# A four-layer image network: involution by columns of tiles and direct 3x3 convolutions, in place of involution by rows of tiles and convolutions by minimal filtering F(4,3)

## The chip, the core and the metric

One of the eight cores of a Trainium2 chip runs the whole network in one program. The metric is the time of that program on the device in microseconds. A core has five engines, each with its own queue of instructions in order: TensorE (PE, matrix products into PSUM; its weight loads are shown as PEld), VectorE (DVE), ScalarE (ACT), GpSimd (POOL) and SyncE (SP, which here only issues transfers). Sixteen DMA engines move data. Tiles live in SBUF, 128 partitions wide. All data is fp32.

## The reference

The image batch `x` is 4 x 256 x 56 x 56. Four layers follow one another, each as `x = x + layer(group_norm(x))`, with 32 groups of 8 channels. Layers 0 and 2 are involutions: a 1x1 bottleneck to 64 channels and a 1x1 span to 16 groups x 49 taps gives every pixel and every group of 16 channels its own 7x7 filter, which is applied to the normalised image. Layer 1 is a block of two 3x3 convolutions of 256 channels. Layer 3 is a gate over a Fourier sum.

```python
# layers 0 and 2 (2 has batch norms and a relu around the same core)
h = jnp.einsum('bchw,oc->bohw', x, reduce_w) + reduce_b[None, :, None, None]
kern = jnp.einsum('bchw,oc->bohw', h, span_w) + span_b[None, :, None, None]
kern = kern.reshape(b, G, 1, K * K, Ho, Wo)
out = (kern * patches).sum(axis=3)          # patches: 7x7 neighbourhoods, pad 3
# layer 1
h = _conv3x3(x, w1, stride=1)
h = jax.nn.relu(_bn(h, g1, b1, rm1, rv1))
h = _bn(_conv3x3(h, w2, stride=1), g2, b2, rm2, rv2)
return jax.nn.relu(x + h)
```

## The kernel before

**Involution** (`involution_layer`, called for layers 0 and 2). The image is cut into tiles of `TY` x `TX` = 3 x 8 output pixels, 19 rows of tiles (`NTY`) by 7 columns (`NTX`), 133 tiles in all (`NT`). A tile's patch has `QY` x `QX` = 9 x 14 = 126 pixels (`Q`). With the patch's 126 pixels on the partitions, the layer is a matrix product per tile: the patch (126 x channels) against a tap matrix (126 x 24 output pixels) for each group of channels.

For an image `b`, `prepare` loads both blocks of 128 channels, takes the statistics (`norm_stats`), and for each block and each column of tiles calls `strip`: ACT writes the normalised 14-pixel-wide strip (L274), PE transposes it in seven pieces of 9 rows (L287), ACT copies these out of PSUM (L290), and POOL's queue stores them to the DRAM scratch `xT` (L293). The seven pieces start at every third row of tiles only; the patches of the other rows of tiles begin inside a piece, which is why the strip goes through DRAM. Then the bottleneck's matmuls (L331) and ACT give `hp`.

`tap_matrices(b, cb)` builds the tile `kt` for one block `cb` of eight groups. It has 32 steps; a step is six matmuls of 64 x 126 weights by 133 columns (L368), three for each of two groups, into two PSUM tiles `k0`, `k1` of two buffers each. An eviction adds the bias and writes `kt`: of every eight PSUM tiles, ACT takes three in three instructions each (L385), DVE five in one each (L392).

`apply(b, cb, kt)` goes by rows of tiles. For each of the 19 rows SP's queue loads the seven patches `xw` from `xT` (L413, four buffers), PE does 7 x 4 matmuls of 126 x 32 weights by 48 columns (L417), and DVE (layer 0, L431) or ACT and DVE (layer 2, L437 to L443) add the result to the residual `res`, which is loaded again from DRAM (L409) and stored by POOL's queue (L445) every five rows of tiles.

The next image's `prepare` is woven by hand into `apply`: `weave` alternates two generators by their shares of steps. Within this order a scheduler places the instructions on the engines' queues, and pools with a fixed number of buffers make a writer wait until the readers of the old content are done.

**Convolutions** (`conv_layer`). They go by minimal filtering F(4,3) along the image's rows: four neighbouring output pixels from six input values take six products instead of twelve. The weights are transformed once (L489 to L499). For stripes of 18 to 20 image rows, `input1` and `input2` make the six transformed inputs on DVE (`transform`, 12 instructions per block), `products` multiplies them (6 products of 6 matmuls, L580) and combines them to four outputs on ACT and DVE (L592 to L603). `conv1` and `conv2` evict; `conv2` reloads the residual and stores the output.

**Gate** (`gate_layer`): as before and after.

Of the kernel before, what the change touches and what calls it, by code (L numbers as in the profile page):

```python
# [45 lines left out]
RES_TY = 5  # L46


WT, WPOS = W // 4, 6
CV_ROWS = 20  # L50
C1_ROWS = [(0, 20), (20, 38), (38, 56)]
C2_ROWS = [(0, 19), (19, 37), (37, 56)]
# [32 lines left out]
def net_kernel(  # L85
# [35 lines left out]

    xT = [dram.tile([NB, NTX, HS * QX, P], F32, name=f"xT{i}") for i in range(2)]
# [53 lines left out]

    def norm_stats(xb, mm_ps):
# [32 lines left out]
    def involution_layer(layer, xin, xout, red, span, sb):  # L210
        with ExitStack() as es:
# [6 lines left out]


# [5 lines left out]
            taps = work.tile([P, NB, KK * KK, GB], F32, name="taps", bufs=1)  # L225
# [15 lines left out]
            bias_g = work.tile([G, KK, KK], F32, name="bias_g", bufs=1)  # L241
# [3 lines left out]
            bias_f = work.tile([G, ZN], F32, name="bias_f", bufs=1)  # L245
# [14 lines left out]

            h_of = {}

            def strip(b, xs, rstd, shift, cb, tx):

                st = work.tile([P, HS, QX], F32, name="strip")
# [6 lines left out]
                if at + hi - lo < QX:  # L272
# [3 lines left out]
                    xs[:, cb, :].rearrange("p (h w) -> p h w", w=W)[:, :, lo:hi],  # L276
# [5 lines left out]
                xts = work.tile([Q, NSB, P], F32, name="xts")  # L282
                for k in range(0, NSB, 4):
                    n = min(4, NSB - k)
                    ps = mm_ps.tile([P, 512], F32, name="mm")
                    for i in range(n):
                        nc.tensor.transpose(  # L287
                            ps[:Q, i * P : (i + 1) * P], flat[:, (k + i) * Q : (k + i + 1) * Q], ident_sb
                        )
                    nc.scalar.copy(  # L290
                        xts[:, k : k + n, :], ps[:Q, : n * P].rearrange("q (n c) -> q n c", n=n)
                    )
                nc.gpsimd.dma_start(xT[b % 2][cb, tx].rearrange("(n q) c -> q n c", q=Q), xts)  # L293

            def prepare(b):

                xs = big.tile([P, NB, HW], F32, name="xs")
                for cb in range(NB):
                    nc.sync.dma_start(xs[:, cb, :], xin[b][cb])
                yield  # L300
                rstd, shift = yield from norm_stats(xs, mm_ps)

                redn = work.tile([P, NB, 2 * R], F32, name="redn")
# [15 lines left out]
                yield  # L319
                for cb in range(NB):  # L320
                    for tx in range(NTX):
                        strip(b, xs, rstd, shift, cb, tx)
                        yield

                hp = big.tile([P, TY, TX, NTY, NTX], F32, name="hp")
                nc.gpsimd.memset(hp[:, TY - 1, :, NTY - 1, :], 0.0)
                for j in range(-(-H // ROWS_H)):
                    rows = min(ROWS_H, H - j * ROWS_H)
                    ps = mm_ps.tile([P, 512], F32, name="mm")
                    for ci in range(NB):  # L330
# [3 lines left out]
                            xs[:, ci, j * ROWS_H * W : (j * ROWS_H + rows) * W],  # L334
# [16 lines left out]
                h_of[b] = hp  # L351


            PREP1, PREP2 = 1 + 2 * NCHUNK + 2 + 1 + NTX, NTX + 7

            def tap_matrices(b, cb):

                hp = h_of[b]
                kt = big.tile([Q, NT, GB, TP], F32, name="kt")
                n = 0  # L360
                for gp in range(GB // 2):
                    for pb in range(TP // PB):
                        ps = [k_ps.tile([P, 512], F32, name=f"k{i}") for i in range(2)]
                        for k in range(PB):
                            py, px = divmod(pb * PB + k, TX)
                            z0 = ZF - py * QX - px
                            for i in range(2):
                                nc.tensor.matmul(  # L368
                                    ps[i][:Q, k * NT : (k + 1) * NT],
                                    z_sb[  # L370
                                        i * R : (i + 1) * R,
                                        cb * GB // 2 + gp,
                                        z0 : z0 + Q,
                                    ],
                                    hp[i * R : (i + 1) * R, py, px].rearrange("p a t -> p (a t)"),
                                    start=True,
                                    stop=True,
                                )
                        for i in range(2):
                            gl = 2 * gp + i  # L380
                            g = cb * GB + gl
                            p0 = pb * PB
                            if n % 8 in (1, 4, 6):
                                for k in range(PB):
                                    nc.scalar.activation(  # L385
                                        kt[:, :, gl, p0 + k],
                                        ps[i][:Q, k * NT : (k + 1) * NT],
                                        AF.Identity,
                                        bias=zb_sb[:, g, p0 + k : p0 + k + 1],
                                    )  # L390
                            else:
                                nc.vector.tensor_tensor(  # L392
                                    kt[:, :, gl, p0 : p0 + PB].rearrange("q t k -> q k t"),
                                    ps[i][:Q, : PB * NT].rearrange("q (k t) -> q k t", k=PB),
                                    zb_sb[:, g, p0 : p0 + PB].unsqueeze(2).to_broadcast([Q, PB, NT]),
                                    ALU.add,
                                )
                            n += 1
                return kt

            def apply(b, cb, kt):

                xt = xT[b % 2]
                for c0 in range(0, NTY, RES_TY):
                    ntr = min(RES_TY, NTY - c0)
                    y0 = c0 * TY
                    rows = min(H, (c0 + ntr) * TY) - y0
                    res = work.tile([P, RES_TY * TY * W], F32, name="res", bufs=3)
                    nc.sync.dma_start(res[:, : rows * W], xin[b][cb][:, y0 * W : (y0 + rows) * W])  # L409
                    for ty in range(c0, c0 + ntr):  # L410
                        xw = work.tile([Q, NTX, P], F32, name="xw", bufs=4)
                        q0 = ty * TY * QX
                        nc.sync.dma_start(xw, xt[cb, :, q0 : q0 + Q, :].rearrange("t q c -> q t c"))  # L413
                        ps = o_ps.tile([P, 2, TY, W], F32, name="o")
                        for tx in range(NTX):
                            for j in range(GB // 2):
                                nc.tensor.matmul(  # L417
                                    ps[32 * j : 32 * j + 32, :, :, tx * TX : (tx + 1) * TX],
                                    xw[:, tx, 32 * j : 32 * j + 32],
                                    kt[:, ty * NTX + tx, 2 * j : 2 * j + 2, :].rearrange(  # L420
                                        "q g (y x) -> q g y x", y=TY
                                    ),
                                    start=True,
                                    stop=True,
                                )
                        n = min(TY, H - ty * TY)
                        xs = res[:, (ty - c0) * TY * W : ((ty - c0) * TY + n) * W]
                        o = [ps[:, i, :n, :].rearrange("p y w -> p (y w)") for i in range(2)]
                        if layer == 0:
                            for i in range(2):  # L430
                                nc.vector.scalar_tensor_tensor(  # L431
                                    xs, o[i], par_sb[:, i : i + 1], xs, ALU.mult, ALU.add
                                )
                        else:
                            u = work.tile([P, TY * W], F32, name="u", bufs=3)
                            un = u[:, : n * W]
                            nc.scalar.activation(  # L437
                                un, o[0], AF.Identity, bias=t4[:, cb : cb + 1], scale=s4p[:, 0, cb : cb + 1]
                            )
                            nc.vector.scalar_tensor_tensor(  # L440
                                un, o[1], s4p[:, 1, cb : cb + 1], un, ALU.mult, ALU.add
                            )
                            nc.vector.scalar_tensor_tensor(xs, un, 0.0, xs, ALU.max, ALU.add)  # L443
# [405 lines left out]
```

## Time and profile before

| | us |
|---|---|
| median of 3 runs | 2649.42 |
| lowest, highest | 2646.02, 2665.11 |
| the profiled execution | 2649.42 |
| its span, first to last instruction | 2647.6 |

The mean granted clock of TensorE is 0.857 of full speed. In the page's 40 slices of the span (66 us each, busy time in tenths), the layers can be told apart: slices 1 to 12 are layer 0, 13 to 25 the convolutions, 26 to 37 layer 2, the last three the gate.

```profile
PE   4777777777771999999999996587777677866422
DVE  2445644654565767667667564164365265445544
ACT  2435444444230412313313210355555455533311
PEclk8788889888785999999999998598888889877666
DMA  4385486568556101102101013327756945775353
```

The costliest groups (line, engine, operation, written tile, read tiles, shape, count; then busy us and mean ns of one; then idle time before them and who ended it):

```profile
L580 PE MATMUL mm<-v,u_sb 128*128 128x252 f32 (+2 forms) x3456 | 765.9, 384 | 5.7 <-DVE v L525 5.7
L368 PE MATMUL k<-hp,z_sb 64*126 64x133 f32 x6144 | 548.2, 302 | 100.2 <-DVE kt L392 67.4
L392 DVE TENSOR_TENSOR kt<-k,zb_sb 126x399 f32<-126x399 f32 x640 | 483.6, 832 | 216.3 <-PE k L368 207.4
L385 ACT ACTIVATE kt<-k,zb_sb 126x133 f32<-126x133 f32 x1152 | 378.8, 473 | 288.8 <-PE k L368 244.5
L417 PE MATMUL o<-kt,xw 126*32 126x48 f32 x17024 | 322.7, 235 | 205.6 <-issue 141.5
L287 PE MATMUL mm<-ident_sb,strip 128*126 128x128 f32 x784 | 174.1, 369 | 90.8 <-ACT xts L290 44.8
```

An fp32 matmul of the source appears as two records. A group's mean duration counts the overlap of pipelined neighbours; busy time over count is the pace. The transfers by queue (packets, MB, share of sixteen engines' span), and the two large issues (KB each, us to landing where the trace has it):

```profile
q1 hardware_dynamic: 293392, 246.69, 33.7%
q0 software_dynamic: 24192, 89.18, 10.3%
...
xw<-xT SPq DMA_DIRECT2D x304, 441.0 KB
xT<-xts POOLq DMA_DIRECT2D x112, 441.0 KB, 7.6
```

### The profile page before, as it was taken

What the parts mean: (1) busy time and instruction counts of PE and PEld (TensorE: products, weight loads), DVE (VectorE), ACT (ScalarE), POOL (GpSimd) and SP (SyncE); (2) the same over time, 40 slices, a digit from 0 to 9 for tenths busy, and PEclk for the clock granted to TensorE, in tenths of its full rate; (3) what the DMA queues carried; (4) which work ended last, traced back from release to release, by engine and by line L of the source; (5) the groups of instructions that cost most, each with busy time, mean ns of one, the idle gap of its engine ahead of it and who ended that gap; (6) DMA issues with size and microseconds to landing.
All of it is one profiled execution on the core that took longest, in us unless ns stands there. A gap on an engine that the chain in (4) does not pass through costs nothing. (4 is left out here: it accounts for less than half of the span.)

```text
span 2647.6 us, 63963 instructions
## 1 busy us (share of the span) xinstructions
PE 1993.9 (75%) x27984; PEld 1607.9 (61%) x27984; DVE 1433.6 (54%) x2911; ACT 958.7 (36%) x2158; POOL 295.4 (11%) x531
## 2 busy tenths in 40 slices
PE   4777777777771999999999996587777677866422
PEld 3556655665661788888888885465566466655100
DVE  2445644654565767667667564164365265445544
ACT  2435444444230412313313210355555455533311
POOL 2111011011001000000000000201101101100235
PEclk8788889888785999999999998598888889877666
DMA  4385486568556101102101013327756945775353
GB/s 127 124 202 160 145 229 185 140 182 228 124 142 194 49 17 66 65 17 74 57 33 65 1 34 116 110 79 213 198 141 168 249 130 163 193 176 139 151 197 145
DMA packets 325518, 346.15 MB, mean 131 GB/s; under 512 B 14483, under 2 KB 288115, under 8 KB 320627
## 3 DMA queue, kind: packets, MB, share of 16 engines
q1 hardware_dynamic: 293392, 246.69, 33.7%
q0 software_dynamic: 24192, 89.18, 10.3%
q10 hardware_dynamic: 7654, 6.19, 0.8%
q8 instruction: 220, 3.60, 0.6%
q14 instruction: 60, 0.48, 0.1%
HBM read 239.91 MB, written 102.06 MB: 129 GB/s over the span
## 5 line engine op out<-in xcount | busy, mean ns | idle before, releaser
L580 PE MATMUL mm<-v,u_sb 128*128 128x252 f32 (+2 forms) x3456 | 765.9, 384 | 5.7 <-DVE v L525 5.7
L580 PEld LDWEIGHTS mm<-v,u_sb 128*128 128x128 f32 x3456 | 655.0, 190 | 114.0 <-issue 5.7
L368 PE MATMUL k<-hp,z_sb 64*126 64x133 f32 x6144 | 548.2, 302 | 100.2 <-DVE kt L392 67.4
L392 DVE TENSOR_TENSOR kt<-k,zb_sb 126x399 f32<-126x399 f32 x640 | 483.6, 832 | 216.3 <-PE k L368 207.4
L368 PEld LDWEIGHTS k<-hp,z_sb 64*126 64x126 f32 x6144 | 463.8, 196 | 179.7 <-DVE kt L392 121.0
L385 ACT ACTIVATE kt<-k,zb_sb 126x133 f32<-126x133 f32 x1152 | 378.8, 473 | 288.8 <-PE k L368 244.5
L417 PE MATMUL o<-kt,xw 126*32 126x48 f32 x17024 | 322.7, 235 | 205.6 <-issue 141.5
L417 PEld LDWEIGHTS o<-kt,xw 126*32 126x32 f32 x17024 | 271.1, 130 | 295.0 <-issue 226.9
L431 DVE SCALAR_TENSOR_TENSOR res<-o,par_sb,res 128x168 f32<-128x168 f32 (+1 forms) x304 | 117.0, 389 | 269.8 <-PE o L417 260.4
L287 PE MATMUL mm<-ident_sb,strip 128*126 128x128 f32 x784 | 174.1, 369 | 90.8 <-ACT xts L290 44.8
L440 DVE SCALAR_TENSOR_TENSOR u<-o,s4p,u 128x168 f32<-128x168 f32 (+1 forms) x152 | 59.1, 389 | 269.2 <-ACT u L437 269.1
L290 ACT COPY xts<-mm 126x512 f32<-126x512 f32 x224 | 112.4, 533 | 222.8 <-DMA xT<-xts 134.3
L287 PEld LDWEIGHTS mm<-ident_sb,strip 128*126 128x126 f32 x784 | 121.4, 188 | 114.1 <-issue 95.1
L274 ACT ACTIVATE strip<-xs,shift,rstd 128x784 f32<-128x784 f32 (+1 forms) x112 | 113.2, 1015 | 110.1 <-DVE shift L201 91.2
L293 POOL DMA_DIRECT2D xT<-xts x112 | 113.8, 1016 | 189.1 <-ACT xts L290 183.4
L437 ACT ACTIVATE u<-o,bn_t,s4p 128x168 f32<-128x168 f32 (+1 forms) x152 | 74.0, 489 | 151.5 <-PE o L417 148.9
L555 ACT ACTIVATE ph<-xb,shift,rstd 128x294 f32<-128x294 f32 (+2 forms) x96 | 79.7, 893 | 125.3 <-DVE shift L201 103.7
L331 PE MATMUL mm<-xs,redn 128*128 128x504 f32 (+1 forms) x224 | 111.5, 634 | 11.5 <-ACT xts L290 10.1
L612 ACT ACTIVATE ph<-y,bn_t,bn_s 128x252 f32<-128x252 f32 (+1 forms) x96 | 55.3, 602 | 134.4 <-DVE y L602 96.7
L445 POOL DMA_DIRECT2D x<-res x64 | 36.6, 571 | 448.6 <-DVE res L443 188.6
L183 DVE BATCH_NORM_STATS2 st<-xb 128x6 f32<-128x448 f32 x112 | 61.9, 609 | 39.2 <-DMA xb<-x 39.2
L183 DVE BATCH_NORM_STATS2 st<-xs 128x6 f32<-128x448 f32 x112 | 64.1, 602 | 28.9 <-DMA xs<-x 14.6
(109 smaller groups left out, 1258.0 us busy)
## 6 DMA issues: line engine op xcount, KB each, us to landing
xw<-xT SPq DMA_DIRECT2D x304, 441.0 KB
xT<-xts POOLq DMA_DIRECT2D x112, 441.0 KB, 7.6
xb<-x SPq DMA_DIRECT2D x16, 1568.0 KB
x<-res POOLq DMA_DIRECT2D x48, 420.0 KB, 7.3
xs<-in_x_dram SPq DMA_DIRECT2D x8, 1568.0 KB
xs<-x SPq DMA_DIRECT2D x8, 1568.0 KB
out_dram<-xb SPq DMA_DIRECT2D x16, 784.0 KB
res<-in_x_dram SPq DMA_DIRECT2D x24, 420.0 KB
```

Of the source, the lines that this page charges most:

```text
L183: nc.vector.bn_stats(st[:, j, :], xb[:, cb, j * CR * W : (j + 1) * CR * W])
L274: nc.scalar.activation(st[:, PAD : PAD + H, at : at + hi - lo], xs[:, cb, :].rearrange("p (h w) -> p h w", w=W)[:, :, lo:hi], AF.Identity, ...
L287: nc.tensor.transpose(ps[:Q, i * P : (i + 1) * P], flat[:, (k + i) * Q : (k + i + 1) * Q], ident_sb)
L290: nc.scalar.copy(xts[:, k : k + n, :], ps[:Q, : n * P].rearrange("q (n c) -> q n c", n=n))
L293: nc.gpsimd.dma_start(xT[b % 2][cb, tx].rearrange("(n q) c -> q n c", q=Q), xts)
L331: nc.tensor.matmul(ps[:, : rows * W], redn[:, ci], xs[:, ci, j * ROWS_H * W : (j * ROWS_H + rows) * W], start=(ci == 0), stop=(ci == NB - 1),)
L368: nc.tensor.matmul(ps[i][:Q, k * NT : (k + 1) * NT], z_sb[i * R : (i + 1) * R, cb * GB // 2 + gp, z0 : z0 + Q,], hp[i * R : (i + 1) * R, p ...
L385: nc.scalar.activation(kt[:, :, gl, p0 + k], ps[i][:Q, k * NT : (k + 1) * NT], AF.Identity, bias=zb_sb[:, g, p0 + k : p0 + k + 1],)
L392: nc.vector.tensor_tensor(kt[:, :, gl, p0 : p0 + PB].rearrange("q t k -> q k t"), ps[i][:Q, : PB * NT].rearrange("q (k t) -> q k t", k=PB) ...
L417: nc.tensor.matmul(ps[32 * j : 32 * j + 32, :, :, tx * TX : (tx + 1) * TX], xw[:, tx, 32 * j : 32 * j + 32], kt[:, ty * NTX + tx, 2 * j : ...
L431: nc.vector.scalar_tensor_tensor(xs, o[i], par_sb[:, i : i + 1], xs, ALU.mult, ALU.add)
L580: nc.tensor.matmul(ps[:, : n * WT], u[:, ci, dy, k, co * P : (co + 1) * P], v[:, k, ci, dy * WT : (dy + n) * WT], start=(i == 0), stop=(i ...
```

## The change

Two layers' worth of code change together.

The involution goes by columns of tiles. The scratch `xT` is gone. `strip` now leaves its seven transposed pieces in SBUF as the first 7 of 19 windows of `xw` (four buffers, made four columns ahead), and fills the other 12 windows with four copies from SBUF to SBUF on SP's queue, shifted by 42 and by 84 partitions. `apply` takes one column of tiles: 19 x 4 matmuls into two PSUM tiles of 10 and 9 rows of tiles. The result is added in place into the loaded image `xs` (three buffers, one block each), which is stored as a whole after its seven columns. `tap_matrices` has one PSUM tile of two halves per step (two buffers), and of every four steps ACT evicts one (six instructions) and DVE three (two each). The statistics are taken by block (`block_stats`). The next image's loads, statistics and bottleneck stand at fixed places between the columns; the next strip follows each column.

The convolutions are direct: nine taps x two input blocks, 18 accumulating matmuls of 448 columns (8 image rows), read from a padded image `xpad`; the first convolution writes its result in place, two rows higher, and the second reads it there.

```diff
-    xT = [dram.tile([NB, NTX, HS * QX, P], F32, name=f"xT{i}") for i in range(2)]
...
             def strip(b, cb, tx):
...
-                xts = work.tile([Q, NSB, P], F32, name="xts")
+                xw = work.tile([Q, NTY, P], F32, name="xw", bufs=NXW)
...
-                nc.gpsimd.dma_start(xT[b % 2][cb, tx].rearrange("(n q) c -> q n c", q=Q), xts)
+                n = NSB - 1
+                for j in range(1, TY):
+                    cut = TY * QX * j
+                    at = window(j)
+                    nc.sync.dma_start(xw[: Q - cut, at : at + n, :], xw[cut:Q, 0:n, :])
+                    nc.sync.dma_start(xw[Q - cut : Q, at : at + n, :], xw[:cut, 1 : 1 + n, :])
+                return xw
...
             def tap_matrices(b, cb):
...
-                        ps = [k_ps.tile([P, 512], F32, name=f"k{i}") for i in range(2)]
+                    ps = k_ps.tile([P, 2, 512], F32, name="k")
...
-                            if n % 8 in (1, 4, 6):
+                    if n % 4 == 2:
+                        for i in range(2):
+                            for k in range(PB):
+                                nc.scalar.activation(
+                                    kt[:, :, g0 + i, p0 + k],
...
+                    else:
                         for i in range(2):
...
+                            nc.vector.tensor_tensor(
+                                kt[:, :, g0 + i, p0 : p0 + PB].rearrange("q t k -> q k t"),
...
+            def apply(b, cb, kt, tx, xw):
+                img = xs_of[b, cb].rearrange("p (h w) -> p h w", w=W)
+                for t0 in range(0, NTY, O_TY):
+                    n = min(O_TY, NTY - t0)
+                    ps = o_ps.tile([P, 2, O_TY * TP], F32, name="o")
+                    for ty in range(t0, t0 + n):
+                        at = (ty - t0) * TP
+                        for j in range(GB // 2):
+                            nc.tensor.matmul(
+                                ps[32 * j : 32 * j + 32, :, at : at + TP],
+                                xw[:, window(ty), 32 * j : 32 * j + 32],
+                                kt[:, ty * NTX + tx, 2 * j : 2 * j + 2, :],
...
+                    dst = img[:, t0 * TY : t0 * TY + rows, tx * TX : (tx + 1) * TX]
...
+                            nc.vector.scalar_tensor_tensor(
+                                dst, o[i], par_sb[:, i : i + 1], dst, ALU.mult, ALU.add
+                            )
...
+            for cb in range(NB):
+                run(norm(0, cb))
+            for _ in range(NXW):
+                next_strip()
+            run(bottleneck(0))
+            for u, (b, cb) in enumerate(units):
+                nxt = iter(())
+                if cb == 0 and b + 1 < B:
+                    load(b + 1, 0)
+                    nxt = norm(b + 1, 0)
+                kt = tap_matrices(b, cb)
+                if cb == 1 and b + 1 < B:
+                    load(b + 1, 1)
+                    run(norm(b + 1, 1))
+                    nxt = bottleneck(b + 1)
+                for tx in range(NTX):
+                    apply(b, cb, kt, tx, xws[u * NTX + tx])
+                    next_strip()
+                    for _ in take(nxt, 2 if cb == 0 else 1):
+                        pass
+                run(nxt)
+                nc.gpsimd.dma_start(xout[b][cb], xs_of[b, cb])
...
     def conv_layer(xin, xout):
...
-            def transform(v, ci, ph, n):
...
-            def products(v, u, co, n):
...
+            def conv_group(xp, w_sb, co, row0):
+                ps = mm_ps.tile([P, 512], F32, name="mm")
+                for n in range(NB * 9):
+                    ci, tap = divmod(n, 9)
+                    dy, dx = divmod(tap, 3)
+                    nc.tensor.matmul(
+                        ps[:, : CR * W],
+                        w_sb[:, ci, tap, co * P : (co + 1) * P],
+                        xp[:, ci, row0 + dy : row0 + dy + CR, PAD - 1 + dx : PAD - 1 + dx + W],
+                        start=(n == 0),
+                        stop=(n == NB * 9 - 1),
+                    )
+                return ps
...
+                for j in range(NCHUNK):
+                    done = []
+                    for co in range(NB):
+                        done.append(conv_group(xp, wc_sb[0], co, j * CR + PAD - 1))
+                    for co in range(NB):
                         nc.scalar.activation(
...
+                for j in range(NCHUNK):
+                    for co in range(NB):
+                        ps = conv_group(xp, wc_sb[1], co, j * CR)
...
+            run(prepare(0))
             for b in range(B):
...
+                    weave(conv_block(b), 2 * NCHUNK, prepare(b + 1), 2 * NCHUNK + 6)
```

## The prediction

> **What bounds the kernel now.** I read the page's totals, cut the span into stages by the first and last matmul of each layer, then looked inside the stages.
>
> ```profile
> span 2647.6 us, 63963 instructions
> PE 1993.9 (75%) x27984; PEld 1607.9 (61%) x27984; DVE 1433.6 (54%) x2911; ACT 958.7 (36%) x2158; POOL 295.4 (11%) x531
> ```
>
> TensorE (PE) leads on average, which says little: the stages differ. Busy time by stage (start:end, length, then PE, weight load, DVE, ACT, POOL, granted clock, DMA share, GB/s):
>
> ```profile
> 99.70:811.00 711.30, 533.51 (x11986) 429.83 (x11986) 379.69 (x699) 289.13 (x763) 73.81 (x171) 0.85 0.63 170
> 811.00:865.00 54.00, 1.17 (x4) 1.00 (x4) 32.06 (x52) 3.96 (x5) 7.99 (x5) 0.50 0.52 183
> 865.00:1632.00 767.00, 766.51 (x3468) 656.60 (x3468) 526.27 (x1239) 193.90 (x308) 17.41 (x41) 1.00 0.12 44
> 1632.00:1738.00 106.00, 50.36 (x191) 37.58 (x192) 15.55 (x46) 35.16 (x62) 21.18 (x56) 0.60 0.44 132
> 1738.00:2451.00 713.00, 530.50 (x11982) 426.42 (x11978) 371.30 (x697) 360.48 (x913) 73.89 (x172) 0.85 0.64 170
> ```
>
> Three facts. The convolution (865 to 1632) is TensorE without a gap, at full clock: its length is its matmul columns. Each involution layer spends 100 or 106 us in a lead-in (0 to 99.7 is layer 0's) and 711 or 713 us in eight rounds of tap matrices and apply. The gate layer (2451 to the end) is 197 us.
>
> Inside the rounds two phases alternate. An apply phase (same columns):
>
> ```profile
> 142.50:195.00 52.50, 34.52 (x1117) 27.30 (x1119) 15.64 (x46) 14.64 (x22) 10.57 (x27) 0.78 0.94 238
> ```
>
> The transfers are busy 94% and TensorE waits at a clock of 0.78: the path through DRAM (xT written, xw read) is the limit. The timeline of a tap phase (start, length, idle before):
>
> ```profile
> 2034.60 1.63 PE L368 MATMUL k<-hp,z_sb 64*126 64x133 f32 x22 [0.18 <-DVE kt L392]
> 2036.43 2.37 PE L368 MATMUL k<-hp,z_sb 64*126 64x133 f32 x26 [0.20 <-ACT kt L385]
> ...
> 2038.98 1.63 PE L368 MATMUL k<-hp,z_sb 64*126 64x133 f32 x22 [0.18 <-DVE kt L392]
> ```
>
> Four steps take 4.38 us (2034.60 to 2038.98): PE, DVE and ACT are balanced, each waiting 0.2 to 0.4 us for another. 32 steps make 35 us. The tap phases of layer 0, from first to last L392, last 40.7, 34.2, 46.3, 33.9, 44.1, 34.4, 33.9 and 37.8: mean 38.2, so an apply phase is 88.9 - 38.2 = 50.7.
>
> **Convolution.** A matmul in the source is two in the trace (3456 records of L580 for 1728). Before: 56 rows x 14 tiles = 784 columns per image and output block, x 36 (6 products of 6 matmuls) x 16 (2 blocks, 2 convolutions, 4 images) = 451,584 columns, at 766.5/451,584 = 1.697 ns. After: 7 chunks x 448 columns x 18 matmuls x 16 = 903,168: exactly double, 1533 us. What leaves is the transforms and products on DVE (526 us busy) and ACT, hidden under TensorE already: worth nothing. Bounds of the price per column: from the forms 252 (369.5 us/864 matmuls = 427.7 ns) and 266 (259.5/576 = 450.5) the slope is 1.63 and 448 columns cost 747 ns, 1506 us; from the widest fp32 matmul, L331 with 504 columns at 1.89 us for two, 1.875 ns, 1693 us. I take 1533, the same operation. The new convolution has evictions of only one ACT per 18 matmuls in the first convolution and an ACT and two DVE in the second, with 6 PSUM buffers against 13.7 us per group (18 x 0.760): hidden. The next image's normalisation is woven in, in the other padded buffer: hidden; if its cover fails, one norm is about 10 us, four times.
>
> The lead-in of 54 us loses 24 weight transforms on DVE at 0.95 (23 us, partly beside loads), keeps 12 weight DMAs, and gains two zero fills of 7688 columns on POOL (6.5 each by the 5.9 us of 6960), and a wait for the last 1.6 MB store that holds the memory. I take 50, between 36 and 65. Tail 5. Stage: 821 becomes 50 + 1533 + 5 = 1588, **+767**.
>
> **Involution lead-in.** Before, 14 strips went through DRAM ahead of the first tap: the first strip starts at 39.4, taps at 99.7. After: 4 strips, then the bottleneck. Statistics come a little later as they run one block after the other (3 us) and image 1's are queued in front on DVE (7 x 0.6, partly in gaps): 44. Strips cost ACT 1.05 + 0.58 + 0.48 = 2.1 each, half hidden under the second block's statistics: 4. The 14 bottleneck matmuls took 13.6 in layer 2's lead-in (1722.7): sum 62, **-38** per layer.
>
> **Tap phase.** Same matmuls, other evictions: of four steps DVE takes three (6 halves) and ACT one (2), before 5 halves and 3; and a step's PSUM pair is now one tile with two buffers, so step n+2 cannot start before both halves of n are out. Walk of four steps from rows: DVE pair 1.52, 12 matmul records 0.82, DVE to PE 0.18, PE to DVE 0.16, six ACT 1.91. DVE: step 0 from 0 to 1.52, step 1 to 3.04. Step 3 needs step 1's buffer: PE 3.22 to 4.04, DVE 4.20 to 5.72. Step 2 is ACT's, from about 2.2 to 4.1 (at the latest 4.6), so step 4's matmuls run from 4.3 to 5.1 and DVE takes them at 5.72. Period **5.72** for 4.38: DVE idles 1.16 in each. 8 x 5.72 = 46; with the statistics (7 x 0.6 on DVE, mostly in the idle) 49 in every second one. Lower bound: 35, nothing lengthens.
>
> Does the clock hold in those idle pieces? In apply phases seven transposes took 0.95 us after a gap of 1.31 (248.70) but 1.73 after one of 1.20 (241.50), and the lowest granted clock in the table is 0.50. At half clock four steps are 4 x 1.64 = 6.56, the phase 53, 16 x 7 = 112 more in all; I keep 46, since PE stays over half busy, and 53 as the bound.
>
> [...]
>
> Behind the waiting matmul stand on PE only the rest of the phase and a few transposes; DVE is who waits for it, as walked.
>
> **Apply phase.** PE work is unchanged: per column of tiles 152 records at 0.80/56 = 2.17, plus 7 transposes 0.98. Seven columns are 22, and in the second phase of an image the next bottleneck adds 12.5 (6 x 1.96 + 0.7): 34.6. At the clock of 0.85 that these layers had: 26 and 41. Beside it, per column: DVE 4 x 0.45 = 1.8; ACT 2.1, and in layer 2 two more of 0.55 with DVE 2.6: below 3.7. The shifts are four copies on SP's queue, 252 runs of 3 KB, 774 KB. Nothing in this trace copies SBUF to SBUF. By queue q1's rate (246.69 MB in 33.7% of 16 engines, 276 GB/s) a column takes 2.8 us, 20 a unit: hidden. By the store xT, 7.6 us for 441 KB on a loaded queue, 13.3 us, 93 a unit: not hidden. I take 2.8, since transfers fall from 16.3 MB a unit (3.1 + 8.4 + 3 x 1.6) to 8.6 and the apply phase holds only the shifts; four buffers give three columns (11 us) for latency. On SP's queue the load of the next block waits for the last store, and shifts queue behind it, but during the tap phase with four columns ready: nothing. The output stays in the input tile, so its reload vanishes; on POOL 112 issues for xT (1.02 each) and 64 stores go and 16 stores come, so its zero fills of the strips come earlier, and nothing waits for them.
>
> [...]
>
> Per image: 46 + 26 + 49 + 41 and 1.5 for each change of phase pair = 165; four images 660, less 18 for the last (no bottleneck or statistics): 642, against 711 and 713. With lead-ins, layer 0 goes 811 to 704 (62 + 642) and layer 2 819 to 710 (68 + 642): **-216**. Gate layer: 0, its tiles only change pool.
>
> **Sum.** 2647.6 + 767 - 216 = 3199; the run was 2649.42, 1.8 around the span, and is itself the median: **3200 us**.
>
> **Rivals.**
> - Taps do not lengthen (PE starts a step as soon as half a buffer is free, or DVE runs gapless at 6 x 0.755 = 4.53): 36 a phase, 16 x 10 = 160 less, about 3040. For it: the old period was well balanced; against: the single tile per step. Chance 0.17.
> - The shifts bind the apply phase: from 3.7 us a column in the first phase and 5.9 in the second. At 6 us, 8 x (16 + 1) = 136 more, 3335; at the bound of 13.3, 4150. For: they are unseen, four to a column; against: DMA is idle 37% already at twice the bytes. Chance 0.2.
> - Not slower: wide matmuls at a lower price. It decides at (766.5 + 216)/903,168 = 1.09 ns a column; at half, 0.85 ns, the convolution stays 767 and the time is 2433. Against it: the two forms of L580 cost 1.697 and 1.694, and L331, twice as wide, 1.875. Chance 0.02. Nor can the involution pay instead: at the fast records its TensorE work is 16 x (26 + 22) + 8 x 12.5 = 868 of 1630 us, so even without any wait or lead-in it gives 762, less than 767.
> - That the words hide an unchanged convolution is excluded: the diff issues 18 matmuls per group over all 112 groups.
>
> **Chances.** Forecast 0.6, the rivals 0.17, 0.2 and 0.02, rest 0.01. From the unknowns: taps -176 to +112, apply -83 (full clock) to the shifts' +136, conv -27 to +160. Not all fall together: 3010 to 3370. Slower by over 1% 0.97, faster by over 1% 0.02, within 1% (what a measurement here cannot tell from nothing) 0.01.
>
> **What would show it.** L565 near 1533 us busy with 1.00 clock; four tap steps at 5.7 us with DVE idle 1.2 us in each four; apply phases near 26 and 41 with DMA share below 0.9; first tap near 62. I am wrong if PE waits for xw copies in apply, if four steps take 4.5, or if a column of L565 is not 1.7 ns.

## The result and the profile after

| | before | after |
|---|---|---|
| median, us | 2649.38 | 3239.95 |
| lowest, highest | 2646.02, 2665.11 | 3234.72, 3245.39 |
| ratio, 95% interval | | 1.2215 [1.2163, 1.2267] |
| span of the profiled execution | 2647.6 | 3243.6 |

The changed kernel is slower by 590.6 us. The forecast was 3200 in a range of 3010 to 3370. First the totals of the page of the changed kernel (busy us, share of the span, instructions):

```profile
span 3243.6 us, 63468 instructions
PE 2637.2 (81%) x28592; PEld 1618.1 (50%) x28592; DVE 1035.8 (32%) x1839; ACT 707.6 (22%) x1550; POOL 182.6 (6%) x411
```

DVE fell from 1433.6 to 1035.8 us and PE rose by 643. The stages say where. Busy time of the changed kernel by stretch (start:end, length, then PE, weight load, DVE, ACT, POOL, granted clock, DMA share, GB/s): lead-in and rounds of layer 0, lead-in and matmuls of the convolution, lead-in and rounds of layer 2, gate.

```profile
0.00:66.10 66.10, 33.21 (x134) 24.40 (x136) 19.12 (x76) 17.00 (x35) 7.16 (x29) 0.97 0.39 130
66.10:747.00 680.90, 494.23 (x12054) 400.20 (x12052) 401.08 (x691) 230.87 (x598) 21.74 (x131) 0.93 0.28 90
747.00:781.30 34.30, 1.23 (x6) 1.03 (x5) 13.19 (x32) 1.81 (x2) 14.43 (x5) 0.52 0.91 361
781.30:2311.70 1530.40, 1530.40 (x4044) 761.85 (x4044) 95.91 (x174) 107.54 (x127) 35.77 (x74) 1.00 0.04 13
2311.70:2364.20 52.50, 29.88 (x136) 21.23 (x137) 19.02 (x58) 17.43 (x34) 4.46 (x18) 0.67 0.45 158
2364.20:3044.00 679.80, 484.37 (x12053) 388.81 (x12051) 394.33 (x693) 291.59 (x710) 22.43 (x134) 0.94 0.29 93
3044.00:3243.60 199.60, 63.93 (x176) 20.56 (x176) 93.13 (x116) 41.42 (x45) 76.60 (x20) 0.62 0.41 162
```

The fourth line is the loss: the convolution's matmuls are gapless at full clock, as before, and last 1530.4 us instead of 767.0. DVE's work beside them fell from 526.3 to 95.9 us, nearly all that it lost in the whole kernel, and bought nothing there. The involution rounds take 680.9 and 679.8 us where they took 711.3 and 713.0, at less than half the DMA share. The costliest groups (line, engine, operation, tiles, shape, count; busy us and mean ns; idle before them and who ended most of it):

```profile
L565 PE MATMUL mm<-xp,wc_sb 128*128 128x448 f32 x4032 | 1530.6, 541 | 7.1 <-ACT xp L550 7.1
L404 PE MATMUL k<-hp,z_sb 64*126 64x133 f32 x6144 | 512.9, 301 | 216.3 <-DVE kt L424 174.5
L424 DVE TENSOR_TENSOR kt<-k,zb_sb 126x399 f32<-126x399 f32 x768 | 559.4, 830 | 193.2 <-PE k L404 192.7
...
L441 PE MATMUL o<-kt,xw 126*32 126x48 f32 x17024 | 284.1, 217 | 144.9 <-issue 122.4
```

The tap matmuls now idle 216 us instead of 100, most of it until DVE has read a buffer. The apply matmuls idle 145 us, 122 of them until "issue", that is, until nothing that the page names. Two steps of a walk follow. The timeline of DVE in a tap phase (start, length, instructions, idle before):

```profile
685.32 4.37 DVE L424 TENSOR_TENSOR kt<-k,zb_sb 126x399 f32<-126x399 f32 x6 [1.14 <-PE k L404]
690.82 4.35 DVE L424 TENSOR_TENSOR kt<-k,zb_sb 126x399 f32<-126x399 f32 x6 [1.14 <-PE k L404]
```

Six evictions, then 1.14 us of waiting for PE: four steps take 690.82 - 685.32 = 5.50 us, before 4.38. And two apply phases, the second and the first of an image (columns as above):

```profile
548.00:587.30 39.30, 34.89 (x1146) 24.63 (x1148) 12.32 (x29) 18.62 (x40) 2.13 (x14) 1.00 0.43 136
459.90:496.70 36.80, 24.48 (x1098) 21.34 (x1098) 13.51 (x35) 11.06 (x18) 1.83 (x12) 0.90 0.43 127
```

The first line is 4 us longer than its PE work, the second 12. That second line is what the forecast missed (it said 26). The end of layer 2 shows the idle time by itself, in the timeline of PE, where no strip and no shift is left to make:

```profile
3023.01 1.74 PE L441 MATMUL o<-kt,xw 126*32 126x48 f32 x127 [2.08 <-issue]
3026.67 1.30 PE L441 MATMUL o<-kt,xw 126*32 126x48 f32 x100 [1.93 <-issue]
3028.21 0.53 PE L441 MATMUL o<-kt,xw 126*32 126x48 f32 x27 [0.24 <-DVE u L462]
3030.62 1.60 PE L441 MATMUL o<-kt,xw 126*32 126x48 f32 x125 [1.89 <-issue]
```

Every 125 to 127 matmul records (the second stretch is 100 + 27, with a short wait for DVE in it) PE stops for 2 us. The page's queues say what is that regular: the queue of instructions moved 226 packets, 3.70 MB, 16.4 KB each. Shared over 2 x 28592 records of PE (matmuls and weight loads) this is 64.7 bytes a record, so one packet holds some 128 matmul records with their loads:

```profile
q1 hardware_dynamic: 42832, 157.58, 14.5%
q0 software_dynamic: 5888, 38.54, 3.2%
...
q8 instruction: 226, 3.70, 0.5%
```

The theory to test: in apply phases PE waits for its own code. Its rival: PE or the buffers wait for the shift copies.

### The profile page after: what moved, and what is told of

Its sections match the earlier page's. It is cut to its first block, busy times and chain, and to the rows that moved or that the text cites. A ratio compares the mean times of both kernels' runs of the same rounds, so it can differ in the third digit from the quotient of the medians.

```text
span 3243.6 us, 63468 instructions
## 1 busy us (share of the span) xinstructions
PE 2637.2 (81%) x28592; PEld 1618.1 (50%) x28592; DVE 1035.8 (32%) x1839; ACT 707.6 (22%) x1550; POOL 182.6 (6%) x411
## 3 DMA queue, kind: packets, MB, share of 16 engines
q1 hardware_dynamic: 42832, 157.58, 14.5%
## 4 chain that ended last, share of the span: by engine, by line
PE 57%; DVE 10%; issue 4%; DMA 3%; POOL 2%; ACT 1%; SPq 0%; POOLq 0%; ACTq 0%; DVEq 0%
PE mm L565 47%; DVE kt L424 8%; PE o L441 4%; PE k L404 2%; POOL xb L724 2%; PE mm L325 1%; PE mm L372 1%; DMA xb<-x 1%; DVE st L174 1%; DMA sfb<-sf 1%; DMA xs<-x 1%; DVE st L200 0%; DMA wc_sb<-in_wc_dram 0%; PE mm L664 0%; DMA x<-xs 0%
## 5 line engine op out<-in xcount | busy, mean ns | idle before, releaser
L565 PE MATMUL mm<-xp,wc_sb 128*128 128x448 f32 x4032 | 1530.6, 541 | 7.1 <-ACT xp L550 7.1
L565 PEld LDWEIGHTS mm<-xp,wc_sb 128*128 128x128 f32 x4032 | 760.1, 189 | 772.9 <-issue 765.7
L424 DVE TENSOR_TENSOR kt<-k,zb_sb 126x399 f32<-126x399 f32 x768 | 559.4, 830 | 193.2 <-PE k L404 192.7
L441 PE MATMUL o<-kt,xw 126*32 126x48 f32 x17024 | 284.1, 217 | 144.9 <-issue 122.4
L441 PEld LDWEIGHTS o<-kt,xw 126*32 126x32 f32 x17024 | 243.0, 116 | 211.7 <-issue 175.8
L415 ACT ACTIVATE kt<-k,zb_sb 126x133 f32<-126x133 f32 x768 | 229.5, 478 | 498.7 <-PE k L404 498.7
L453 DVE SCALAR_TENSOR_TENSOR xs<-o,par_sb,xs 128x240 f32<-128x240 f32 x224 | 98.8, 450 | 176.0 <-PE o L441 153.7
L328 ACT COPY xw<-mm 126x512 f32<-126x512 f32 x224 | 110.5, 535 | 173.3 <-PE mm L325 144.1
L311 ACT ACTIVATE strip<-xs,sh,rs 128x784 f32<-128x784 f32 (+1 forms) x112 | 113.9, 1019 | 81.4 <-DVE sh L191 80.5
L462 DVE SCALAR_TENSOR_TENSOR u<-o,s4p,u 128x240 f32<-128x240 f32 x112 | 50.2, 450 | 181.8 <-ACT u L459 181.5
L459 ACT ACTIVATE u<-o,bn_t,s4p 128x240 f32<-128x240 f32 x112 | 59.7, 538 | 102.6 <-PE o L441 99.5
L724 POOL TENSOR_TENSOR xb<-xb,xn 128x1568 f32<-128x1568 f32 x16 | 73.8, 4639 | 32.3 <-DVE xn L721 32.3
```

The source lines that it names most:

```text
L311: nc.scalar.activation(st[:, PAD : PAD + H, at : at + hi - lo], xs_of[b, cb].rearrange("p (h w) -> p h w", w=W)[:, :, lo:hi], AF.Identity, ...
L328: nc.scalar.copy(xw[:, k : k + n, :], ps[:Q, : n * P].rearrange("q (n c) -> q n c", n=n))
L415: nc.scalar.activation(kt[:, :, g0 + i, p0 + k], ps[:Q, i, k * NT : (k + 1) * NT], AF.Identity, bias=zb_sb[:, cb * GB + g0 + i, p0 + k : p ...
L424: nc.vector.tensor_tensor(kt[:, :, g0 + i, p0 : p0 + PB].rearrange("q t k -> q k t"), ps[:Q, i, : PB * NT].rearrange("q (k t) -> q k t", k ...
L441: nc.tensor.matmul(ps[32 * j : 32 * j + 32, :, at : at + TP], xw[:, window(ty), 32 * j : 32 * j + 32], kt[:, ty * NTX + tx, 2 * j : 2 * j ...
L453: nc.vector.scalar_tensor_tensor(dst, o[i], par_sb[:, i : i + 1], dst, ALU.mult, ALU.add)
```

## The experiments

Kernels ran on different chips, so single runs are compared by their **excess** over the kernel before on the same chip; after's is 590.6 us. Seven executions of before on one chip spread from 2642.32 to 2662.13 us, so a difference of single runs below some 20 us says little. Phase lengths are from the last L424 of one tap phase to the first of the next (apply), and from first to last (tap).

**Without the shift copies.** `window()` returns the seven transposed pieces for all rows of tiles; the shift of the patches is left out.

```diff
-                for j in range(1, TY):
...
                 k, j = divmod(ty, TY)
-                return (0, NSB, 2 * NSB - 1)[j] + k
+                return k
```

> The changed kernel without the four shift copies per column of tiles; each row of tiles reads the nearest of the seven transposed pieces, so the shifting of the patches is left out of the computation. Theory A (PE waits for its own code: the stalls called issue fall every 127 to 133 records, not at a wait): they stay, L441 keeps over 100 us of issue idle, the first apply phase of an image stays at 33 to 37 us, time 3190 to 3245. Theory B (the shift copies, as queue time or as landing, hold the columns at 5.6 us): the first apply phases fall from 37 to about 25 and the second from 39 to 35, 8 x 15 = 120 less: about 3120.

Measured: 3156.20 beside 2638.55, an excess of 517.7, 73 less. An image's first apply phase fell from 32 to 39 us to 30.6 to 31.6, and the waits of PE for its code did not vanish (line waited for: us, times, longest):

```profile
PE o L435 <- issue: 83.3, 75, 2.3
```

In after it is 122.4 us in 83 waits, the longest 3.3. So neither theory holds whole: the stops are there with no shift copy in the kernel, and with the copies they are longer (1.47 us in the mean for 1.11).

**Half the apply matmuls.** Weights of 64 columns instead of 32, so 38 matmuls per column of tiles instead of 76; only the first two of every four groups' filters are used.

```diff
-                        for j in range(GB // 2):
+                        for j in range(GB // 4):
                             nc.tensor.matmul(
-                                ps[32 * j : 32 * j + 32, :, at : at + TP],
-                                xw[:, window(ty), 32 * j : 32 * j + 32],
-                                kt[:, ty * NTX + tx, 2 * j : 2 * j + 2, :],
+                                ps[64 * j : 64 * j + 64, :, at : at + TP],
+                                xw[:, window(ty), 64 * j : 64 * j + 64],
+                                kt[:, ty * NTX + tx, 4 * j : 4 * j + 2, :],
```

> The changed kernel with half as many apply matmuls: 64 columns of weights instead of 32, 38 matmuls per column of tiles instead of 76, the same 48 moving columns; each block of 64 channels uses only the tap matrices of its first two groups, so two of four groups' filters are left out. The shift copies stay. Theory A (code): half the records per column, the issue idle of L441 falls below 40 us, the first apply phase to 24 to 29 us, time 3240 less 70 to 130. Theory B (shift copies): the columns stay at 5.6 us and the phases at 37, time 3225 to 3245.

Measured: 3085.65, an excess of 447.1, 144 less. The group of the apply matmuls, from this kernel's page:

```profile
L441 PE MATMUL o<-kt,xw 126*64 126x48 f32 x8512 | 298.1, 224 | 3.0 <-DVE xs L453 1.5
```

Half the records are as long in sum (298 us against 284), so PE had the same work; the idle time fell from 144.9 to 3.0 us, by 142 beside a gain of 144. The instruction queue moved 160 packets instead of 226. A first apply phase is now nothing but its PE work (window of layer 0's first):

```profile
105.90:129.40 23.50, 23.38 (x537) 21.07 (x536) 13.05 (x33) 12.16 (x22) 2.03 (x14) 1.00 0.57 168
```

All shift copies of the phase run beside those 23.5 us, and PE waits for none: the copies keep up. The first phases take 22.4 to 23.5 us, below the 24 to 29 expected of theory A, and the gain is above its 70 to 130.

Half the matmuls is also half of whatever else goes by their number. The trace of after tells these apart, for its record of the instruction queue (q8) has the time of every packet. At the end of layer 2 packets ran from 3020.55 to 3021.48, 3024.35 to 3025.39 and 3028.02 to 3029.29 us; the stops shown above end at 3023.01, 3026.67 and 3030.62. Each of the 83 stops before L441 ends 1.2 to 1.6 us after the end of a packet, each after a different one. And counted in PE's own instructions (matmuls, weight loads and the few others), all 83 end at the same place of a stretch of 256, within two. The 79 stops before L417 in the kernel before do the same (1.2 to 1.8 us). So these waits are for code.

**The tap phase in three steps.** First the pair tile as in after, with before's share of evictions (of eight halves ACT three, DVE five):

```diff
-                    if n % 4 == 2:
-                        for i in range(2):
+                    for i in range(2):
+                        g = cb * GB + g0 + i
+                        if (2 * n + i) % 8 in (1, 4, 6):
...
-                    else:
-                        for i in range(2):
-                            g = cb * GB + g0 + i
+                        else:
```

> The changed kernel with the evictions of the tap matrices shared as before (of eight halves ACT takes three, DVE five), the pair of halves still one PSUM tile. As the prediction's step had it, the single tile per step makes the long cycle: 5.0 to 5.5 us per four steps, time 3190 to 3240. Rival, the order of evictions alone makes it (three DVE steps in a row wait for one buffer): 4.4 to 4.6 us per four steps, tap phases 7 us shorter, 16 x 7 = 112 less: 3100 to 3140.

Measured: 3262.95, an excess of 624.4, 34 more than after; a tap phase without statistics takes 47.1 us (after 44.0). The time is longer than either expectation had it (3190 to 3240, 3100 to 3140): the share alone gains nothing. Its waits show two readers of one tile taking turns:

```profile
ACT kt L416 <- DVE kt L423: 246.2, 120, 7.5
DVE kt L423 <- ACT kt L416: 184.1, 132, 1.9
```

The two engines read different halves, 512 fp32 apart, and still one waits for the other. With a tile for each half and the same share (the last of the three runs) no wait between the two is in the list. What the two runs show is that in this program the order goes by tile: 430 us of such waits with one tile of two halves, none listed with two tiles. With a shared tile, the share of after (a step's two halves to one engine) is the better one.

Then two PSUM tiles per step, with after's share, and last two tiles with before's share:

```diff
-                    ps = k_ps.tile([P, 2, 512], F32, name="k")
+                    ps = [k_ps.tile([P, 512], F32, name=f"k{i}") for i in range(2)]
...
-                                ps[:Q, i, k * NT : (k + 1) * NT],
+                                ps[i][:Q, k * NT : (k + 1) * NT],
```

> The changed kernel with two PSUM tiles per step as before (each half is free when its own eviction is done), the evictions still one ACT step of four. As the prediction's step had it: 4.5 to 4.7 us per four steps, about 16 x 6 = 96 less, 3130 to 3170. Rival, the order of evictions: 5.3 to 5.5 us as now, time 3220 to 3245.

> The changed kernel with both parts of the old eviction: two PSUM tiles per step and of eight halves three on ACT, five on DVE. If the two parts work together (split tiles let ACT and DVE read a step side by side, which one tile does not): 4.4 us per four steps, pure tap phases 35 to 36 us instead of 44, with statistics about 41, 16 x 8.5 = 136 less than the changed kernel: 3090 to 3120. If the split alone is all there is (40.6 in the run with split tiles): phases at 40, 3150 to 3170.

Measured: 3158.56 (excess 520.0, 71 less) and 3104.76 beside 2650.60 (454.2, 136 less). Tap phases without statistics fell from 44.0 to 40.6 and then to about 35, the length of before. The timeline of DVE in the first of the two:

```profile
662.11 4.23 DVE L424 TENSOR_TENSOR kt<-k,zb_sb 126x399 f32<-126x399 f32 x6 [0.83 <-PE k L404]
667.16 4.23 DVE L424 TENSOR_TENSOR kt<-k,zb_sb 126x399 f32<-126x399 f32 x6 [0.83 <-PE k L404]
```

Four steps take 5.05 us, not the 4.5 to 4.7 expected: a buffer of its own for each half gives 0.45 of the 1.12 back, and sharing the work 5 to 3 on top of it the rest. So the longer tap phase has the two causes that the walk named, the single tile and the six halves on DVE; taking away the second alone made it worse.

**One half of the change at a time.** After's involution with the old convolution, and the old involution with the direct convolution:

```diff
-            def conv_group(xp, w_sb, co, row0):
...
+            def transform(v, ci, ph, n):
...
+            def products(v, u, co, n):
```

> The changed involution with the old convolution by F(4,3). If the two halves of the change add up: layers 0 and 2 as in the changed kernel (747 and 732 us instead of 811 and 819), the convolution stage 821 again: 2649 - 151 = 2498, ratio 0.94 (2475 to 2520). If the involution's gain is an effect of the other convolution layer beside it (its memory, its lead-in): 2600 to 2650.

> The old involution by rows with the direct convolution. If the halves add up: 2649 + 1565 - 821 = 3393 (3370 to 3415). A convolution stage dearer or cheaper than 1565 by over 20 us would say that its lead-in depends on what stands before it.

Measured: 2516.72 (2506.95 to 2522.56), ratio 0.9499 [0.9462, 0.9536], 134 us less than before; and 3390.89, 740 us more. The sum, 606, is the 591 of both together within 16 us: the halves hardly act on each other, and they pull in opposite directions. With the old involution ahead of it the direct convolution has the same lead-in as in after (34 us) and the same matmuls (1531.0 us busy).

**The better halves together.** After's involution, its taps with two tiles and before's share, and the old convolution, so the edits of two runs above.

> The changed involution with the old eviction of the tap matrices (both parts) and the old convolution. If all three add up: 2498 - 136 = 2362, ratio 0.89 (2340 to 2390). If the tap phases are held by something else once the cycle is short: 2420 to 2500.

Measured: 2376.17 (2372.67 to 2378.27), ratio 0.896 [0.8933, 0.8988]. This beats both kernels. From its page:

```profile
span 2370.9 us, 63584 instructions
PE 1873.0 (79%) x28016; PEld 1532.3 (65%) x28016; DVE 1407.8 (59%) x2799; ACT 943.2 (40%) x2118; POOL 158.1 (7%) x379
...
L446 PE MATMUL o<-kt,xw 126*32 126x48 f32 x17024 | 272.5, 216 | 127.2 <-issue 117.6
```

Its apply phases still stop for code, 118 us in all: what is left there.

**More traffic beside the apply phase.** After, with one more copy per column of tiles that nobody reads:

```diff
+                nc.sync.dma_start(xd[tx % 4], xw[:, NSB:NTY, :])
                 return xw
```

> After, with one more copy of 774 KB per column of 12 windows, from the window buffer to a scratch buffer in DRAM, on SP's queue; nothing reads it. Theory A (PE waits for its own instructions at each 16 KB, and transfers lengthen those waits): the idle time before L441 that the profile puts down to nothing rises from 122 us to 150 to 170, an image's first apply phase grows from 36 to 40 to 42 us, the time goes to about 3320 us. Theory B (what cost time was PE or the buffers waiting for the shift copies, so that a copy that nobody waits for is free): about 3240 us, first phases 36 to 37.

Measured: 3263.63 beside 2643.26, an excess of 620.4, 30 more; first apply phases of layer 0 took 36.3 to 42.1 us, those of layer 2 34.1 to 38.2. The waits of the apply matmuls for code hardly moved:

```profile
PE o L443 <- issue: 127.9, 83, 3.5
```

Both numbers expected were wrong: 80 us more was expected of theory A, none of theory B. Of the 30 us, 13 are waits until "issue" (122.4 to 127.9 before the apply matmuls, 8.2 to 15.5 before the transposes), 12 are tap matmuls that wait longer for DVE and ACT. So "bytes lengthen the stops" is not a law: taking the shift copies away saved 39 us of stops, adding as many bytes to DRAM cost 13. What it is in the copies within SBUF (by the code 252 runs a column for 126, the write side, the queue's order) is open.

**Half the apply matmuls in the kernel before.** The same edit on `apply` by rows (groups left out as above).

```diff
-                            for j in range(GB // 2):
+                            for j in range(GB // 4):
...
-                                    ps[32 * j : 32 * j + 32, :, :, tx * TX : (tx + 1) * TX],
+                                    ps[64 * j : 64 * j + 64, :, :, tx * TX : (tx + 1) * TX],
```

> Before, with half the matmuls of the apply phase: weights of 64 columns, of which only the first two of four groups' filters are taken; it leaves out the other groups' filters. Theory A (the apply phases of before are bound by the transfers through DRAM, as the prediction took them): they stay at 50 to 53 us and the time at 2620 to 2650. Theory B (PE's own instructions hold them up as they do in after): they fall to 45 us or less, and the time by 80 us or more.

Measured: 2581.11 beside 2643.26, 62 less; apply phases with a strip in them went from 46 to 56 us to 45 to 51, between the two expectations. What PE waited for in them changed places. Before, and with half the matmuls:

```profile
PE o L417 <- issue: 141.5, 79, 5.9
...
PE o L417 <- DMA xw<-xT: 47.2, 51, 2.8
```

```profile
PE o L417 <- DMA xw<-xT: 126.3, 108, 4.3
```

The stops for code before the apply matmuls went, and 79 us more of waiting for patches from DRAM came in their place. Both limits stood close behind each other; the forecast saw the one and took no note of the other, though its 141.5 us stand in the trace of before, in the list of what PE waited for.

## Why the prediction was right, point by point

**Convolution: right.** The step "exactly double, 1533 us" at 1.697 ns a column measured 1530.4, which over 903,168 columns is 1.694. The DVE and ACT work that left was indeed worth nothing, and the new evictions are hidden (idle before L565: 7.1 us). The lead-in, taken as 50, was 34.3: too high by 16, and the tail of 5 did not come. Alone, the direct convolution cost 740 us (forecast 767).

**Involution lead-ins: one right, one too long.** 66.1 for 62, but 52.5 for 68.

**Tap phase: right in mechanism and size.** The walk gave 5.72 us for four steps with DVE idle 1.16; measured are 5.50 and 1.14, phases of 44.0 for 46. The lengthening by statistics was put on "every second one"; in fact five or six of the eight phases of a layer take 47 to 51, so the eight of layer 0 sum to 380 us for 377. The two causes were shown by the split tile and, on top of it, the share. The clock held, as the window of layer 0's first tap phase shows:

```profile
66.10:110.10 44.00, 31.89 (x399) 25.68 (x397) 34.86 (x48) 15.27 (x49) 0.42 (x3) 1.00 0.00 1
```

The clock in it is 1.00, so the 112 us at half clock, kept as a bound, did not come. The reason given for 46, that PE stays over half busy, was the author's estimate and no run shows such a limit: PE was 72% busy here, and in the old apply phase 66% at a clock of 0.78.

**Apply phase: mechanism incomplete, term mis-sized.** "Seven columns are 22 ... 26 and 41" (27.5 and 42.5 with the change of phase). Measured: 36.0 in the mean for the first phase of an image, 40.6 for the second. PE's work was near what was worked out at full clock (24.5 for 22 and 34.9 for 34.6 in the windows shown), and the clock was 0.90 and 1.00 there, not 0.85. So the two wrong parts of the term, a clock too low and no stops, work against each other: in the second phase they cancel by luck (40.6 for 42.5), and in the first the stops win by 8.5 us, eight times in two layers. Without stops, with half the matmuls, the first phase takes 23 us, not 26. The step that failed is "PE work is unchanged", followed by a sum of PE's work at the old clock: it left out the 141.5 us that the old apply matmuls already waited for "issue". They were put down to the transfers as a whole.

**Shift copies: hidden as a wait, not as a cost.** PE never waited for `xw` copies, and 2.8 us a column of transfer time was about right: with and without them queue q1 differs by 14.5% of 3243.6 less 5.8% of 3154.3 = 287 us, 2.6 for each of 112 columns. Yet they cost 73 us: 39 by longer stops for code, the rest in shares that weren't separated. That is half of the rival "the shifts bind the apply phase" (136), by another way than the one named. The rival "taps do not lengthen" fell with the 5.50, the one on cheap wide matmuls with the 1.694 ns.

**The sum.** Layer 0 came to 747 for 704: lead-in +4, taps +3, apply +36. The convolution came to 1565 for 1588, layer 2 to 732 for 710 (lead-in -16, taps -1, apply +39), the gate to 200 for 197: +43 - 23 + 22 + 3 = +45, hence 3243.6 for the 3199 of the sum. The involution saves 151 us, not 216. That the forecast missed the median by only 40 us is partly luck: the apply term was 75 us too short, and lead-ins and a convolution taken some 35 us too long made up for nearly half of it.

## What to carry to other kernels

When the busiest engine of a stage is one at full clock without a gap, count what the change does to its work there first: cutting DVE's work in the convolution from 526 to 96 us was worth nothing and doubling PE's columns cost 740 us. Before taking an engine's work as the length of a phase, read what ended its idle time there, "issue" too: a limit that stands behind the one you remove becomes the next, as the waits for code did (141.5 us before, 122.4 after). And two engines that read halves of one PSUM tile took turns here (430 us of such waits in the run with the old share); a tile for each half removed that.

## What the runs showed of the hardware

PE's code comes in pieces of 16.4 KB, some 128 matmul records with their weight loads, and a stream of 126x32 weights by 48 columns runs through one faster than the next comes: at the end of layer 2 a piece ran in 1.6 to 1.8 us and the next began 3.7 to 4.0 us after it (3023.01, 3026.67, 3030.62), an estimate of 16.4 KB / 3.8 us = 4.3 GB/s. The packet itself lasts 1.06 us (median of 226), so most of that time is not the moving of its bytes; PE goes on 2.2 to 3.3 us after the packet's begin. In the whole of after no packet begins less than 3.36 us after the one before it, and by the count of instructions none begins more than some 300 instructions ahead of the one that would wait for it. With 64 weight columns a column of tiles is 76 records in 2.42 us:

```profile
112.40 2.42 PE L441 MATMUL o<-kt,xw 126*64 126x48 f32 x76
```

128 records then take an estimated 4.1 us, longer than the 3.8 between two pieces, and the stops vanished. All 226 packets of after have 16,384 bytes, and its 83 stops fall at one place of every 256 of PE's instructions: an estimate of 64 bytes an instruction, beside the 64.7 a record above. The price is about 2 us a piece in such a stream (1.89 to 2.08 in the timeline above) and 122 us in this kernel.
